# A message-passing layer on one core: the order of VectorE's queue around the message product, and the items in which ranks and node features are made

## The chip, the cores and the metric

The kernel runs on one core of a Trainium2 chip. The metric is device time in microseconds (us), the median of three runs. One more execution was taken by the hardware profiler; its trace is what the profile sections read.

The engines are named as the profile names them: PE is TensorE (PEld its weight loads), DVE is VectorE, ACT is ScalarE, POOL is GpSimd, and SP is the queue that issues most loads.

## The reference

One layer over 6250 nodes and 200000 edges, sorted by the node `dst` from which a message comes.

```python
h = relu(layernorm(x))                                        # 6250 x 128
xw = h @ W_in
W_ij = (ssp(edge_attr @ W_f1 + b_f1) @ W_f2 + b_f2) * edge_weight   # 200000 x 128, ssp(v) = softplus(v) - log 2
x_ij = xw[dst] * W_ij                                         # one message for each edge
out = segment_sum(x_ij, src, 6250)                            # src has no order
return x + ssp(out @ W_o1 + b_o1) @ W_o2 + b_o2
```

## The kernel before

The edges are cut into 391 quads of 4 x 128. One loop iteration, called an item here, works on several quads at different depths. Tiles and semaphores are automatic, but the order of the instructions on each engine is the order in which the program writes them (`manual_schedule`), and each engine takes its instructions in that order. Item `i` is written so:

- PE: `s2_pe_x(i-1)` gathers the node rows of quad `i-1` with a one-hot matrix (tile `xg`) and starts `W`, `s2_pe_w(i-1)` finishes `W`, `s1_pe(i+1)` makes `z`. Then come the hooks "PE2".
- ACT: `s1_exp(i)`, `s1_ln(i)`, hooks "A0", hooks "A1", `s2_copy(i-1)` (four copies of `xg` times the edge weight, tile `xc`), and after PE2 the hooks "A2".
- DVE: hooks "D0", `s1_oh(i)`, hooks "D1", hooks "DM", the message product `s2_m(i-1)` = `W` x `xc` (line 524), and after PE2 the hooks "D2".
- POOL: four indirect DMAs for each quad that is scattered, which add message rows into one of four sums in device memory.

A hook is a step that a planner put at an item and a point with `at(i, point, fn, ...)`; steps at the same item and point run in the order in which they were planned.

184 of the 391 quads are "sorted" quads (`mpq`). They are not scattered one by one. Eight of them and nine others make a round of 17 items; sorted quads stand at the offsets 0, 2, ..., 14 of a round. For a sorted quad `q`:

- item q+1: the product is written to `mb`, then `perm_oh` (D2) builds four one-hot matrices `pm` (line 665);
- item q+2: ACT casts `mb` into `pt` (`part_hi`, line 676, and `part_ext`, line 685, at A1), DVE makes the second part of `pt` (`part_lo`, line 680, at D2);
- items q+3 and q+4: PE permutes `pt` with `pm` (`permute`, line 691), ACT takes the results out (`mst`, line 696); rows over the capacity go through `over_pe`, `over_idx`, `over_row`, `over_eq`, `over_sum`, `over_copy`, `over_ji` (line 753), `over_int` (line 757) and one scatter.

Four "units" follow for each round, at the offsets 2, 6, 10 and 14 of the next one. For a unit at item k, `unit_oh` builds its eight one-hot matrices `so` (line 768), four at k-2 and four at k-1, both at D2; `unit_pe` (line 783) runs 64 matmuls into all four PSUM buffers of tag B; `unit_evac` (line 794) adds them to `accT` in D1 of item k+1. Whatever else PE writes to a tag B buffer in item k+1 waits for that.

`pos`, which `perm_oh` compares with, comes from the "ranks" of a round: `rank_group` (lines 597 to 610, DVE), `rank_count` (lines 615 and 619, PE), `rank_own` (lines 630 to 635, DVE), `rank_over` (PE) and `rank_slot` (lines 648 to 658, DVE).

The other quads are scattered. Most are "listed": a window of 16 of them gets its row numbers ahead from `l_eq` (line 373, a DM hook), `l_count` (line 382), `l_dup`, `l_scan`, `l_index` and others, and closes with `l_sum`, `l_copy`, `l_ji` (lines 484 and 485) and `over_int`.

The node rows are made on the way, in 24 groups of 256 nodes, nine items apart: `prep_stat` (lines 189 to 193, DVE), `prep_rs0` (ACT), `prep_norm` (lines 207 to 213, DVE), `prep_tp` (line 222, PE, tile `hps`), `prep_relu` (ACT), `prep_mm` (PE), `prep_x1` (ACT), `prep_rm` (line 247, DVE), `prep_x2` (line 252, ACT) and `prep_x3` (line 258, DVE, with the store to the table). The edge features are split on the way too, every eight items: `fb_1` to `fb_4`.

`clear(i, busy, n)` gives the first item from `i` on, from which `n` items hold no unit. The tail after the loop adds the sums and makes the output.

## Time and profile before

| | |
|---|---|
| median of 3 runs | 2111.23 us (2109.82 to 2115.32) |
| the profiled execution | 2102.09 us |
| its span (first to last instruction) | 2100.2 us |
| mean granted TensorE clock | 0.932 |
| busy: DVE, ACT, POOL | 1762.2, 1537.2, 1601.1 us |
| busy: PE, PEld | 1786.8, 1532.4 us |
| items of the loop begin at | about 30 us (head), end at about 2030 us (then the tail) |

A busy PE in this table is a union of matmul times whose ends are modelled. "Waits" in the profile are idle time of an engine in front of an instruction, put down to what ended last.

### The profile page before, as it was taken

How to read it: one execution, taken by the hardware profiler on the slowest of the kernel's cores; microseconds unless marked ns; L12 is line 12 of the kernel's file. 1: busy time of each engine (PE TensorE's matmuls, PEld its weight loads, DVE VectorE, ACT ScalarE, POOL GpSimd, SP SyncE). 2: the span in 40 equal slices, each digit the busy share in tenths (PEclk: the TensorE clock that was granted, in tenths of full speed). 3: DMA queues.
4: the chain of work that ended last, by engine and by line, in shares of the span. 5: the costliest groups of instructions: out<-in, count | busy, mean ns of one | idle time of the engine just before them, and what ended most of it. 6: DMA issues, size and time to landing. Idle time of an engine off the chain costs nothing. (4 is left out here: it accounts for less than half of the span.)

```text
span 2100.2 us, 52738 instructions
## 1 busy us (share of the span) xinstructions
PE 1786.8 (85%) x17881; PEld 1532.4 (73%) x17881; DVE 1762.2 (84%) x4448; ACT 1537.2 (73%) x4392; POOL 1601.1 (76%) x984
## 2 busy tenths in 40 slices
PE   3579888887987898988988888888999899998966
PEld 2468777776776777877777777777777777887854
DVE  5687988898888898988989889798898888989865
ACT  3568777776776777777778687687877788898824
POOL 3557888786876877788787788788888888888844
PEclk9789999998999999989999999899999999999978
DMA  7886666665765666666676667666666666767649
GB/s 247 213 202 116 131 117 108 132 107 108 127 119 98 126 124 116 107 118 119 125 125 119 115 110 130 104 118 119 119 118 128 109 117 103 132 116 143 113 87 241
DMA packets 378865, 269.16 MB, mean 128 GB/s; under 512 B 96959, under 2 KB 342506, under 8 KB 378594
## 3 DMA queue, kind: packets, MB, share of 16 engines
q1 hardware_dynamic: 242642, 198.09, 33.7%
q0 software_dynamic: 135664, 67.63, 33.0%
q8 instruction: 141, 2.31, 0.5%
q14 instruction: 130, 1.06, 0.2%
q10 hardware_dynamic: 288, 0.07, 0.0%
HBM read 155.30 MB, written 110.31 MB: 126 GB/s over the span
## 5 line engine op out<-in xcount | busy, mean ns | idle before, releaser
L586 POOL DMA_INDIRECT acc<-s,lji x704 | 1180.3, 1677 | 297.3 <-issue 165.3
L514 ACT ACTIVATE xc<-xg,cb 128x128 f32<-128x128 f32 x1564 | 445.8, 369 | 94.3 <-PE xg L501 91.1
L691 PE MATMUL pq<-pt,pm 128*128 128x258 f32 x2944 | 471.6, 306 | 40.4 <-DVE pt L680 9.9
L509 PE MATMUL W<-w,a 128*128 128x128 f32 x3128 | 475.3, 297 | 0.0
L691 PEld LDWEIGHTS pq<-pt,pm 128*128 128x128 f32 x2944 | 401.6, 200 | 66.9 <-ACT mst L696 12.8
L509 PEld LDWEIGHTS W<-w,a 128*128 128x128 f32 x3128 | 398.4, 200 | 43.6 <-issue 5.9
L783 PE MATMUL un<-so,mst 32*128 32x392 f32 x5888 | 346.8, 368 | 60.9 <-DVE pr L630 40.0
L783 PEld LDWEIGHTS un<-so,mst 32*128 32x128 f32 x5888 | 294.1, 199 | 111.4 <-DVE pr L630 44.8
L665 DVE TENSOR_SCALAR pm<-iot,pos 128x576 fp32r<-128x576 f16 x736 | 345.1, 529 | 0.0
L696 ACT CAST mst<-pq 128x258 fp32r<-128x258 f32 x736 | 253.2, 373 | 113.5 <-PE pq L691 95.7
L327 ACT ACTIVATE a<-a,con 128x512 f32<-128x512 f32 x391 | 282.5, 723 | 12.8
L586 POOL DMA_INDIRECT acc<-s,ji x124 | 206.8, 1668 | 97.4 <-ACT ji L567 43.0
L768 DVE TENSOR_SCALAR so<-iot,mst 128x392 fp32r<-128x392 f16 x736 | 272.8, 431 | 1.4 <-PE un L783 1.4
L322 ACT ACTIVATE a<-z 128x512 f32<-128x512 f32 x391 | 236.3, 604 | 30.6 <-PE z L317 21.6
L794 DVE TENSOR_TENSOR accT<-un,accT 128x392 f32<-128x392 f32 x352 | 174.0, 555 | 35.1 <-PE un L783 34.7
L524 DVE TENSOR_TENSOR s<-W,xc 128x512 f32<-128x512 f32 x176 | 120.8, 687 | 95.0 <-ACT xc L514 87.5
L586 POOL DMA_INDIRECT acc<-os,oji x103 | 172.5, 1675 | 35.4 <-issue 17.7
L501 PE MATMUL xg<-wn,oh 63*128 63x128 bf16 x1564 | 160.2, 225 | 19.4 <-ACT xc L514 13.1
L705 PE MATMUL po<-pt,pm 128*64 128x130 f32 (+1 forms) x736 | 143.1, 251 | 37.7 <-ACT mst L696 24.0
L317 PE MATMUL z<-ft,ws 123*128 123x512 bf16 x391 | 154.3, 395 | 18.3 <-DMA ft<-fsd 15.3
L498 PE MATMUL W<-b2rep,onesb 64*128 64x512 bf16 x391 | 157.1, 402 | 0.0
L705 PEld LDWEIGHTS po<-pt,pm 128*64 128x64 f32 (+1 forms) x736 | 120.7, 168 | 47.2 <-ACT mst L696 29.8
(207 smaller groups left out, 2493.8 us busy)
## 6 DMA issues: line engine op xcount, KB each, us to landing
rb<-reld SPq DMA_DIRECT2D x391, 64.0 KB
fsd<-f SPq DMA_DIRECT2D x49, 480.0 KB
sb<-src SPq DMA_DIRECT2D x183, 128.0 KB
ft<-fsd SPq DMA_DIRECT2D x195, 120.0 KB
fb<-in_fB_dram SPq DMA_DIRECT2D x49, 320.0 KB
ft<-fsd SPq DMA_DIRECT2D x195, 80.0 KB
wn<-tab SPq DMA_DIRECT2D x782, 15.8 KB
acc<-s,lji POOLq DMA_INDIRECT x704
```

Source lines behind the costliest of these rows:

```text
L322: nc.scalar.activation(a, st[q]["z"], AF.Exp)
L327: nc.scalar.activation(a, a, AF.Ln, bias=half, scale=0.5)
L509: nc.tensor.matmul(W[:, c, :], st[q]["a"][:, c * P:(c + 1) * P], w2, start=False, stop=(c == 3))
L514: nc.scalar.mul(xc[:, c, :], st[q]["xg"][:, c, :], late["c", q // CQ][:, 4 * (q % CQ) + c:4 * (q % CQ) + c + 1])
L586: nc.gpsimd.indirect_dma_start(out=accs[k][:rows, :], out_offset=bass.IndirectOffsetOnAxis(ap=ji, axis=0), in_=s, in_offset=None, compute_ ...
L665: nc.vector.tensor_scalar(pm[:, c], iot[:, :SLOTS], rk[r]["pos"][:, 4 * j + c:4 * j + c + 1], None, op0=ALU.is_equal)
L691: nc.tensor.matmul(t[:, :PW], mp[q]["pm"][:, c, s * P:(s + 1) * P], pt[:, c], start=(c == 0), stop=(c == 3))
L696: nc.scalar.copy(mp[q]["ms", s], mp[q].pop(("q", s))[:, :PW])
L705: nc.tensor.matmul(o[:, :P + 2], w, pt[:, c, P:PW], start=(c == 0), stop=False)
L768: nc.vector.tensor_scalar(so, iotw[:, :GN], w[:, 2 * P:2 * P + 1], None, op0=ALU.is_equal)
L783: nc.tensor.matmul(ts[g][:, :GN], mp[q]["ms", s][v, k * P:(k + 1) * P], mp[q]["oh"][v], start=(q == qs[0] and k == 0), stop=(q == qs[-1] a ...
L794: nc.vector.tensor_tensor(v, t[:, :GN], v, op=ALU.add)
```

## The change

Every DVE step planned at "D2" now runs in front of DM and the product instead of after PE2. The first half of each unit's one-hot matrices goes to a new point "D3", at the old place of D2; the second half stays at D2 and so moves in front. `over_ji`, `l_ji` and `over_int` run one item later (D0 and A1 of item k+2). The node steps get two starts, `t0` and `t1`, both at items that are neither a unit nor next to one (`calm`), and are pulled apart: the transpose at t0, the matmul at t1, `prep_x2` at A1 of t1+2, `prep_x3` at D0 of t1+3, the load two items earlier. The ranks are planned at such items too: `rank_count` at k, `rank_over` at o. `rank_group`, which stood at offset 12 of a round, stands at offset 11; `rank_count` moves from offset 13 to 12, `rank_over` from 15 to 16. `over_row` and most `l_count` use `calm` as well. Some small tiles (`ldg`, `leq`, `bb`, `wabs`, `wsel`) move from the tags `h` and `rm`, which the node steps use with one buffer, to a tag of their own with three. The loop has two more items at its end.

```diff
-        dg = wk.tile([P, P], F32, tag="h", name="ldg", bufs=1)
+        dg = wk.tile([P, P], F32, tag="eql", name="ldg", bufs=3)
...
-            t0 = prep_start(g)
-            at(t0 - 3, "L", xt_load, g)
-            at(t0 - 1, "D2", prep_stat, g)
-            at(t0, "A1", prep_rs0, g)
-            at(t0, "D2", prep_norm, g)
-            at(t0 + 1, "PE2", prep_tp, g)
-            at(t0 + 2, "A0", prep_relu, g)
-            at(t0 + 2, "PE2", prep_mm, g)
-            at(t0 + 3, "A0", prep_x1, g)
-            at(t0 + 3, "DM", prep_rm, g)
-            at(t0 + 3, "A2", prep_x2, g)
-            at(t0 + 3, "D2", prep_x3, g)
+            t0, t1 = prep_start(g)
+            at(t0 - 5, "L", xt_load, g)
+            at(t0 - 2, "D2", prep_stat, g)
+            at(t0 - 1, "A1", prep_rs0, g)
+            at(t0 - 1, "D2", prep_norm, g)
+            at(t0, "PE2", prep_tp, g)
+            at(t0 + 1, "A0", prep_relu, g)
+            at(t1, "PE2", prep_mm, g)
+            at(t1 + 1, "A0", prep_x1, g)
+            at(t1 + 1, "DM", prep_rm, g)
+            at(t1 + 2, "A1", prep_x2, g)
+            at(t1 + 3, "D0", prep_x3, g)
...
-            i = max(mpq[RKQ * r], 5)
-            at(i - 5, "D2", rank_group, r)
-            k = clear(i - 4, units)
+            i = mpq[RKQ * r]
+            if i < 10:
+                k, o = i - 1, i
+            else:
+                k = max(k for k in range(i - 20, i - 4) if calm(k, units) == k and calm(k + 1, units) <= i)
+                o = calm(k + 1, units)
+            at(k - 1, "D2", rank_group, r)
             at(k, "PE2", rank_count, r)
             at(k + 1, "D0", rank_own, r)
-            k = clear(k + 1, units)
-            at(k, "PE2", rank_over, r)
-            at(k + 1, "D0", rank_slot, r)
+            at(o, "PE2", rank_over, r)
+            at(o + 1, "D0", rank_slot, r)
...
-            at(k + 1, "DM", l_ji, w)
-            at(k + 1, "A2", over_int, ("L", w))
+            at(k + 2, "D0", l_ji, w)
+            at(k + 2, "A1", over_int, ("L", w))
...
-                k = clear(q + 6, units)
+                k = clear(q + 6, units) if q == mpq[-1] else calm(q + 6, units)
                 at(k, "PE2", over_row, q)
                 at(k + 1, "D0", over_eq, q)
-                k = clear(q + 8, units)
+                k = clear(k + 2, units)
                 at(k, "PE2", over_sum, q)
                 at(k + 1, "A0", over_copy, q)
-                at(k + 1, "DM", over_ji, q)
-                at(k + 1, "A2", over_int, q)
+                at(k + 2, "D0", over_ji, q)
+                at(k + 2, "A1", over_int, q)
...
-                at(k - 2, "D2", unit_oh, r, s, 0)
+                at(k - 2, "D3", unit_oh, r, s, 0)
                 at(k - 1, "D2", unit_oh, r, s, 1)
...
-        for i in range(max(NQ + 7, last + 16, r0_end + 2, lend + 24)):
+        for i in range(max(NQ + 7, last + 18, r0_end + 2, lend + 24)):
...
             run(i, "A1")
             if 0 <= i - 1 < NQ:
                 s2_copy(i - 1)
+            run(i, "D2")
             run(i, "DM")
             if 0 <= i - 1 < NQ:
                 s2_m(i - 1)
...
             run(i, "PE2")
             run(i, "A2")
-            run(i, "D2")
+            run(i, "D3")
...
+def calm(i, busy):
+    while i in busy or i + 1 in busy or i - 1 in busy:
+        i += 1
+    return i
...
-    return clear(7 + PREP_GAP * (g - 1), busy, 3) - 1
+    t0 = calm(7 + PREP_GAP * (g - 1), busy)
+    return t0, calm(t0 + 1, busy)
```

More of the change, by code (lines that the diff above doesn't have):

```diff
@@ L465, in l_same @@
     def l_same(j):
-        eq = wk.tile([P, P], F32, tag="rm", name="leq", bufs=1)
+        eq = wk.tile([P, P], F32, tag="eql", name="leq", bufs=3)
         nc.vector.tensor_scalar(eq, mp["L", j].pop("row")[:, :P], idl[:, j:j + 1], None, op0=ALU.is_equal)
@@ L1015, in tile_gnn @@
             at(t0 + 1, "D2", fb_4, b)
-        busy = units | {prep_start(g) + k for g in range(1, NG) for k in range(5)}
+        busy = units | {t + k for g in range(1, NG) for t in prep_start(g) for k in range(2)}
         mid = clear(NQ // 2, busy, 2) - 6 if spread else 0
@@ L1027, in late_bias @@
             nc.vector.tensor_scalar(nbo1, bo1_sb, -1.0, None, op0=ALU.mult)
-            bb = wk.tile([P, 1, P], F32, tag="rm", name="bb", bufs=1)
+            bb = wk.tile([P, 1, P], F32, tag="eql", name="bb", bufs=3)
             nc.vector.tensor_copy(bb[:, 0], bo1_sb.to_broadcast([P, P]))
@@ L1037, in bound_abs @@
         def bound_abs():
-            t_ = wk.tile([K1, P], F32, tag="h", name="wabs", bufs=1)
+            t_ = wk.tile([K1, P], F32, tag="eql", name="wabs", bufs=3)
             nc.scalar.activation(t_, w1f, AF.Abs)
-            v_ = wk.tile([K1, P], F32, tag="rm", name="wsel", bufs=1)
+            v_ = wk.tile([K1, P], F32, tag="eql", name="wsel", bufs=3)
             nc.vector.tensor_copy(v_, con[:K1, 15:16].to_broadcast([K1, P]))
@@ L1127, in tile_gnn @@
                     at(i + k, "DM", l_eq, kk)
-                i = clear(i + 2, units)
+                i = calm(i + 2, units) if w and g < 3 else clear(i + 2, units)
                 at(i, "PE2", l_count, (LB + SW * w) // 4 + g)
@@ L1509, in base_caps @@
             for g in range(1, len(groups)):
-                if prep_start(g) + 3 >= 2 * s - 4:
+                if prep_start(g)[1] + 3 >= 2 * s - 4:
                     ready = groups[g][0]
```

## The prediction

> **What bounds the kernel now.** First the page's busy times and its row of the granted clock.

> ```profile
> PE 1786.8 (85%) x17881; PEld 1532.4 (73%) x17881; DVE 1762.2 (84%) x4448; ACT 1537.2 (73%) x4392; POOL 1601.1 (76%) x984
> PEclk9789999998999999989999999899999999999978
> ```

> No engine is full. PE and DVE tie at 84 to 85%; head and tail are emptier, so in the loop each is near 88%. The chain that ended last is no help: its rows sum to a few per cent and lie in the tail. So the time is set by two engines handing work to each other, and the question is who waits for whom. That is the table of waits:

> ```profile
> DVE s L524 <- ACT xc L514: 87.5, 84, 3.8
> ...
> ACT oji L757 <- DVE ojd L753: 62.1, 41, 3.6
> ...
> PE un L783 <- DVE pr L630: 40.0, 17, 5.0
> ...
> DVE x L258 <- ACT x L252: 39.4, 15, 4.1
> ...
> PE hps L222 <- DVE accT L794: 26.6, 14, 4.6
> ...
> DVE m L524 <- ACT xc L514: 24.5, 16, 6.5
> ...
> DVE mb L524 <- ACT xc L514: 18.3, 23, 1.9
> ```

> Columns: total us, times, longest. DVE's product waits for the scaled copy 87.5 + 24.5 + 18.3 = 130.3 us, in 123 of 391 items. Each of the other rows belongs to a step that the change moves. Then the stretches: two long ones, and two short ones behind a PE wait of the fifth row.

> ```profile
> 120.00:600.00 480.00, 416.91 (x4114) 360.06 (x4115) 411.05 (x1080) 363.48 (x1047) 371.57 (x223) 0.92 0.66 123
> ...
> 1600.00:2030.00 430.00, 397.29 (x4198) 347.15 (x4202) 372.77 (x910) 334.85 (x980) 355.14 (x215) 0.97 0.66 115
> ...
> 427.00:430.70 3.70, 0.96 (x19) 0.71 (x18) 3.70 (x8) 2.14 (x7) 3.09 (x3) 1.00 0.43 36
> 430.70:434.10 3.40, 3.37 (x19) 2.93 (x17) 3.40 (x8) 2.37 (x7) 2.85 (x2) 0.50 0.57 105
> ```

> Columns: PE, PEld, DVE, ACT, POOL busy, granted clock, DMA share, GB/s. In the early stretch, with node steps, PE idles 63 of 480 us and has a clock of 0.92; in the last, without them, 33 of 430 and 0.97. The two short rows show why these go together: PE was idle for most of 3.7 us, and the next 3.4 us have half the clock. The line of the PE timeline there is

> ```profile
> 429.75 0.44 PE L222 MATMUL hps<-idt,xn 128*128 128x128 f32 x2 [2.71 <-DVE accT L794]
> ```

> In the trace's clock record I count 42 such drops between 120 and 2030 us, 218 us together. Eight follow a wait of `hps` for `accT`, eleven stand at a unit of offset 14, where `un` waits for `pr` (2.9 us at 669 us, for one).

> In rounds: from 156.9 to 1121.6 us eleven rounds take 87.7 us each, with about two node groups in a round; from 1205.2 to 1693.6 us six rounds without node groups take 81.4 us.

> **The change, part by part.** The sum is made against the profiled execution, 2102.1 us; the median of the runs, 2111.2, is 9 us above it. Durations:

> ```profile
> L514 ACT ACTIVATE xc<-xg,cb 128x128 f32<-128x128 f32 x1564 | 445.8, 369 | 94.3 <-PE xg L501 91.1
> ...
> L665 DVE TENSOR_SCALAR pm<-iot,pos 128x576 fp32r<-128x576 f16 x736 | 345.1, 529 | 0.0
> ...
> L768 DVE TENSOR_SCALAR so<-iot,mst 128x392 fp32r<-128x392 f16 x736 | 272.8, 431 | 1.4 <-PE un L783 1.4
> ...
> L680 DVE TENSOR_TENSOR pt<-mb,pt 128x512 fp32r<-128x512 f32 x184 | 125.7, 683 | 0.0
> ...
> L676 ACT CAST pt<-mb 128x512 fp32r<-128x512 f32 x184 | 114.0, 620 | 0.9 <-DVE mb L524 0.6
> ```

> *(a) The new order on DVE.* No instruction of weight is added; the product is only queued later. Gain: where it waited, other work now runs. In the item after a sorted quad's product, `part_lo` (0.68 us) stands in front of the next product. Of the 84 waits of `s` (mean 1.04 us) some 20 lie at offset 0, which has no `part_lo`, and keep theirs; the other 64 lose about 0.6 us each, 38 us. `mb`'s 18.3 go wholly under `perm_oh` (345.1 / 184 = 1.88 us). Of `m`'s 24.5 I take 10. Together 66 us.

> Price: a cover is lost. Before, `perm_oh` and often four `so` (272.8 / 184 = 1.48 us) ran on DVE after `mb`, while ACT cast it, and ACT's cast waited for `mb` 0.6 us in the whole run. Now `mb` comes last, 1.9 to 3.4 us later, and ACT's queue stands: cast 0.62, `ext` 0.20, then `xc` (four, 1.14 us in the timeline), 2.0 us until the next product may start. DVE has for that time `part_lo` and some 0.4 us of small steps: 0.9 us is exposed in each of 184 pairs, 166 us at most. What else now stands there takes part of it back: half of the 88 `eql` (1.2 us each), half of the 49 `fb_2` (1.6) and the 24 `prep_stat` (1.0) cover up to 0.9 us each, 92 x 0.9 = 83. The other 83, and 31 us kept at offset 0 (20 waits, 1.57 us on average there), are 114 against 130 now, -16. The ends: -66 if ACT is always ahead and nothing is newly exposed, +36 if nothing covers (166 - 130). **I take -5**, nearer to the upper end than -16, since the ring also holds `exp` up.

> The late product costs PE little. The buffer that `W` of quad j takes was in the built program last held by `W` of quad j-2 in 337 of 390 cases, so PE needs the product of two items ago. The first half of a unit's `so` keeps its place, the second half comes sooner, and the unit waits for it anyway.

> *(b) Node steps.* `prep_x3` stood right behind ACT's `prep_x2`, which stood behind four `xc`; DVE stood for it 39.4 us, with `pm` and `so` for the next unit queued behind. Now the copy is made at A1 an item earlier than x3. That wait goes; DVE is not always the late one, so I take half: **-20**, ends 0 and -39. The transpose leaves the item after a unit; that wait (26.6) goes, but the buffers are free no sooner: the next tag B user there, `permute`, waits instead. `prep_norm` (1.4 us) leaves the unit's item, `prep_stat` (1.0 us) enters it. **-5**, ends +5 and -27. The loads go out two items earlier on SP's queue, in a space of two buffers that was free: nothing. The store goes from D2 of t0+3 to D0 of t1+3, up to four items later; the table is read far behind: nothing.

> *(c) Ranks.* `rank_own` no longer holds a tag B buffer that a unit needs: 40.0 us of PE waits go. But `rank_group` (seven steps, 3.0 us in the timeline at 1011.4) moves to offset 11, where `accT` (2.0) and `perm_oh` (1.9) stand ahead of the product too; that product becomes 3 us later, and behind it on ACT the cast and `xc`, behind those PE's next `xg`. By hand from one unit's end to the next I get the block no shorter than before. **-4**, ends -40 and +46 (23 rounds x 2.0).

> *(d) Late indices.* ACT loses a wait of 62.1 us with `exp` queued behind. ACT is busy 73%, so most of it was slack: **-4**, ends 0 and -30 (half). The one scatter behind it is written at the same item, and POOL waited for it 1.4 us before; it may now wait up to half an item, 103 times at most, with POOL 76% busy: nothing taken, +10 as an end.

> *(e) Clock.* If the eight drops behind `hps` and half of the eleven at offset 14 go, 13 x 5.2 us (218 / 42) at half clock return 13 x 2.6 = 34 us of PE work; PE is the late one for a part of that: **-8**, ends 0 and -34.

> *(f)* Separate buffers for the small tiles: nothing waits on them now but `leq`, 3.7 us: 0. Two more short items in the tail: **+2**.

> Sum: -5 -20 -5 -4 -4 -8 +2 = **-44**: 2058 on the profiled execution, 2067 as the median.

> [...]

> **The rivals.** *Slower: the lost cover.* One mechanism: product last, ACT's cast and copies, next product, in a ring without slack. If DVE sets the pace nearly everywhere, (a) is +36, the ring also delays `exp` and so PE, and (b) to (e) give back half of theirs, some 20: 2102 + 36 - 20 = 2118, as a median 2127. It decides when DVE's waits for the first cast and for `xc` pass together 130 + 39 = 169 us: the waits before plus the gains of (b) to (f). For it: ACT idles only 27%; against it: the 83 us of other work that now stands in the ring.

> *No change: the ranks eat it.* (c) near its end of +46 cancels the -40 of the rest: 2111. For it: PE's `un` waits follow DVE's whole load, which stays.

> *Much faster.* PE's waits go for good, and the clock of the whole loop is that of the last stretch: 13.6% of the time at half clock now, 6% then, 80 us of PE work, of which I count half, with (a) at -30: 2102 - 40 - 30 - 33 (b to d) + 2 = 2001 at the extreme, 2010 as a median; I give it the middle between that and the forecast, 2038.

> *The drops stay.* They come from PE's load over a window, not from the two waits; then (e) is 0: 2075 as a median. For it: several drops stand behind no wait over 1 us. [...]

> **How the numbers follow.** Forecast 0.47 (its own range 2040 to 2098), lost cover 0.23, ranks 0.08, much faster 0.14, drops stay 0.08. A measurement can tell about 0.3%, 6 us. Faster: 0.47 + 0.14 + 0.08, less 0.01 for the forecast's upper end: 0.68. Slower: 0.23. Same: 0.09. The range from 2028 to 2126 leaves out about half of the lost-cover case above and a third of the fastest below.

> **What would show it.** Right: `x <- ACT x`, `oji <- ojd` and `un <- pr` gone from the waits; the product's waits for `xc` near 110 us; a new wait of DVE's `pt` for ACT's cast, of 30 to 80 us; a granted clock near 0.94; rounds with node groups near 85 us. The lost cover shows as `pt` and `s` waits over 169 us and ACT idle in front of its cast of `mb`. The ranks show as PE or ACT idle at offsets 12 to 14. The forecast is wrong if DVE's idle time does not fall, or if it falls and rounds do not shorten.

## The result, and the profile after

The changed kernel is slower: median 2234.11 us (2230.23 to 2241.87, four runs) against 2111.32 us for the kernel before, run beside it; ratio 1.0583, 95% interval 1.0551 to 1.0615. The forecast was 2067 us in a range of 2028 to 2126. The profiled execution took 2230.23 us, its span 2228.4 us, its mean granted clock was 0.891.

The page's busy times, its clock row, and the windows of the loop in the changed kernel (columns as in the prediction):

```profile
PE 1816.0 (81%) x17881; PEld 1579.3 (71%) x17881; DVE 1783.3 (80%) x4448; ACT 1535.6 (69%) x4392; POOL 1581.2 (71%) x984
PEclk9789889898998988989888899898989998999987
```

```profile
120.00:600.00 480.00, 395.79 (x3871) 345.95 (x3870) 394.67 (x1029) 340.01 (x986) 350.84 (x212) 0.88 0.63 119
...
1600.00:2160.00 560.00, 497.53 (x5177) 436.03 (x5177) 471.18 (x1139) 416.34 (x1208) 436.48 (x263) 0.93 0.63 109
```

The instruction counts are those of before, and the busy times of PE, DVE, ACT and POOL moved by 29 us at most. PE, at 0.88 instead of 0.92 in the first stretch, was also idle for 84 us there instead of 63. So the 128 us that the span has grown are mostly waiting, and a slower clock behind it. The table of waits of the changed kernel says for whom:

```profile
ACT dg L725 <- DVE ovs L720: 147.1, 60, 5.6
...
DVE pt L680 <- ACT pt L676: 139.7, 93, 5.4
ACT mst L696 <- PE pq L691: 114.2, 102, 4.1
...
PE po L705 <- ACT mst L696: 70.2, 40, 4.1
...
DVE s L524 <- ACT xc L514: 59.0, 92, 4.1
...
ACT pt L676 <- DVE mb L524: 41.5, 29, 3.0
```

The rows that the prediction wanted gone are gone or small (`un <- pr` and `hps <- accT` gone, `x <- ACT x` 0.5 us, `oji <- ojd` 12.0). In their place stands a first row that the prediction does not have: ACT waits 147.1 us, in 60 places, for `ovs`. Before, that row was a small one:

```profile
ACT dg L725 <- DVE ovs L720: 9.2, 16, 1.5
```

`ovs` is `over_idx`, a DM step of one tiny DVE instruction, and `dg` is `over_dg`, the first hook (A0) of the next item on ACT.

One place of it, in item 12 of a round; DVE, ACT and PE by the timeline (start, duration, and in brackets the idle time in front and its releaser):

```profile
1157.59 0.18 DVE L597 CAST srcf<-srcT_sb 128x32 f32<-128x32 int16 x1
...
1159.87 0.18 DVE L610 CAST ext<-cnt 128x32 bf16<-128x32 f32 x1
1159.95 1.80 DVE L665 TENSOR_SCALAR pm<-iot,pos 128x576 fp32r<-128x576 f16 x4
1161.67 0.15 DVE L720 SCALAR_TENSOR_TENSOR ovs<-mo 128x1 f32<-128x1 f32 x1
```

```profile
1161.86 0.40 ACT L725 ACTIVATE dg<-idt,ovs 128x128 f32<-128x128 f32 x1 [4.55 <-DVE ovs L720]
1162.16 0.28 ACT L728 ACTIVATE ojd<-ovs,con 128x1 f32<-128x1 f32 x1
1162.35 0.62 ACT L696 CAST mst<-pq 128x258 fp32r<-128x258 f32 x2
```

```profile
1162.75 0.38 PE L615 MATMUL rkp<-G,tri 128*128 128x512 bf16 x1 [3.24 <-ACT mst L696]
...
1168.12 2.50 PE L691 MATMUL pq<-pt,pm 128*128 128x258 f32 x8 [4.33 <-DVE pr L630]
```

The chain: seven rank steps and four `pm` (4.1 us) now run on DVE in front of DM; the 0.15 us of `ovs` come behind them; ACT stands 4.55 us in front of `dg`, and in its queue behind `dg` are the `mst` that empty PE's tag B buffers; PE stands 3.24 us for a buffer, later 4.33 us more, until DVE's `pr` has freed the buffer of the ranks' own count; and then, at a granted clock of 0.50, the eight `pq` take 2.50 us, where eight of them take 1.20 us at a granted clock of 1.00 (at 1156.22 us of the same trace).

The length of an item, from the start of one `W` to the next, is worked out from the trace (mean of the rounds 2 to 20, us, by offset in the round; last column: time at half clock between 120 and 2030 us). The rows below `after` are experiments:

| kernel | 4 | 8 | 12 | 16 | all 17 | half clock |
|---|---|---|---|---|---|---|
| before | 3.8 | 4.3 | 4.7 | 4.6 | 84.1 | 218 |
| after | 6.1 | 7.0 | 11.5 | 8.5 | 90.5 | 403 |
| e2 | 5.0 | 5.4 | 7.9 | 6.9 | 85.2 | 239 |
| e8 | 3.9 | 4.7 | 4.9 | 4.7 | 83.2 | 222 |
| e10 | 4.0 | 4.7 | 4.8 | 4.6 | 82.0 | 215 |
| e16 | 4.2 | 5.7 | 5.6 | 5.4 | 82.7 | 215 |
| e6 | 6.2 | 6.4 | 6.6 | 5.9 | 85.5 | 276 |
| e1 | 6.2 | 6.2 | 11.0 | 7.8 | 88.6 | 362 |
| e9 | 3.6 | 4.7 | 9.5 | 7.1 | 85.1 | 249 |
| e13 | 3.9 | 4.8 | 8.3 | 5.5 | 84.1 | 249 |
| e14 | 3.7 | 4.7 | 7.2 | 6.3 | 83.2 | 259 |

The whole loss lies in four items of a round: 4, 8, 12 and 16 are together 15.7 us longer than before, the other thirteen 9.3 us shorter. These are the items that `calm` returns: with units at 2, 6, 10 and 14, only 0, 4, 8, 12 and 16 are neither a unit nor next to one. They are also the items of `q+4` for the sorted quads at offsets 0, 4, 8 and 12, in which PE2 already makes the second half of a permuted quad and its overflow, three tag B results that ACT takes out only at A0 of the next item. The change puts into just these items the ranks' counts (from 13 and 15), most `l_count` and the nodes' `hps` (both from the odd offsets). Of the four `over_row` of a round three stood at 8, 12 and 16 before; the fourth goes from 3 to 4.

### The profile page after: what moved, and what is told of

Same layout as the page of the kernel before. It is cut to its first block, busy times and chain, and to the rows that moved or that the text cites. A ratio compares the mean times of both kernels' runs of the same rounds, so it can differ in the third digit from the quotient of the medians.

```text
span 2228.4 us, 52670 instructions
## 1 busy us (share of the span) xinstructions
PE 1816.0 (81%) x17881; PEld 1579.3 (71%) x17881; DVE 1783.3 (80%) x4448; ACT 1535.6 (69%) x4392; POOL 1581.2 (71%) x984
## 5 line engine op out<-in xcount | busy, mean ns | idle before, releaser
L586 POOL DMA_INDIRECT acc<-s,lji x704 | 1165.5, 1656 | 420.8 <-issue 161.3
L691 PE MATMUL pq<-pt,pm 128*128 128x258 f32 x2944 | 497.5, 318 | 94.6 <-ACT h L228 32.3
L509 PE MATMUL W<-w,a 128*128 128x128 f32 x3128 | 510.6, 313 | 0.0
L691 PEld LDWEIGHTS pq<-pt,pm 128*128 128x128 f32 x2944 | 425.4, 210 | 119.6 <-ACT mst L696 36.9
L514 ACT ACTIVATE xc<-xg,cb 128x128 f32<-128x128 f32 x1564 | 443.8, 367 | 34.3 <-PE xg L501 27.2
L509 PEld LDWEIGHTS W<-w,a 128*128 128x128 f32 x3128 | 430.1, 213 | 46.9 <-issue 13.1
L665 DVE TENSOR_SCALAR pm<-iot,pos 128x576 fp32r<-128x576 f16 x736 | 343.7, 528 | 9.9 <-PE po L706 7.7
L783 PE MATMUL un<-so,mst 32*128 32x392 f32 x5888 | 296.4, 345 | 2.6 <-DVE oeq L738 1.1
L783 PEld LDWEIGHTS un<-so,mst 32*128 32x128 f32 x5888 | 263.0, 184 | 38.4 <-issue 28.9
L768 DVE TENSOR_SCALAR so<-iot,mst 128x392 fp32r<-128x392 f16 x736 | 277.5, 437 | 1.9 <-PE un L783 1.7
L680 DVE TENSOR_TENSOR pt<-mb,pt 128x512 fp32r<-128x512 f32 x184 | 127.2, 691 | 159.3 <-ACT pt L676 139.7
L705 PE MATMUL po<-pt,pm 128*64 128x130 f32 (+1 forms) x736 | 160.2, 274 | 93.4 <-ACT mst L696 70.2
L705 PEld LDWEIGHTS po<-pt,pm 128*64 128x64 f32 (+1 forms) x736 | 135.2, 187 | 107.7 <-ACT mst L696 80.2
L794 DVE TENSOR_TENSOR accT<-un,accT 128x392 f32<-128x392 f32 x352 | 174.4, 558 | 30.8 <-PE un L783 16.7
L524 DVE TENSOR_TENSOR s<-W,xc 128x512 f32<-128x512 f32 x176 | 121.3, 689 | 78.6 <-ACT xc L514 59.0
L501 PE MATMUL xg<-wn,oh 63*128 63x128 bf16 x1564 | 168.3, 234 | 18.7 <-ACT xc L514 16.9
```

What stands on the lines that cost most here:

```text
L509: nc.tensor.matmul(W[:, c, :], st[q]["a"][:, c * P:(c + 1) * P], w2, start=False, stop=(c == 3))
L514: nc.scalar.mul(xc[:, c, :], st[q]["xg"][:, c, :], late["c", q // CQ][:, 4 * (q % CQ) + c:4 * (q % CQ) + c + 1])
L586: nc.gpsimd.indirect_dma_start(out=accs[k][:rows, :], out_offset=bass.IndirectOffsetOnAxis(ap=ji, axis=0), in_=s, in_offset=None, compute_ ...
L665: nc.vector.tensor_scalar(pm[:, c], iot[:, :SLOTS], rk[r]["pos"][:, 4 * j + c:4 * j + c + 1], None, op0=ALU.is_equal)
L691: nc.tensor.matmul(t[:, :PW], mp[q]["pm"][:, c, s * P:(s + 1) * P], pt[:, c], start=(c == 0), stop=(c == 3))
L705: nc.tensor.matmul(o[:, :P + 2], w, pt[:, c, P:PW], start=(c == 0), stop=False)
```

## The experiments

Two theories. *The late index*: the order "D2 in front of DM" makes `over_idx` late, and ACT and PE behind it. *The lost cover*, the prediction's rival: the product last, ACT's cast and copies and the next product form a ring without slack, whatever stands at DM. The parts that the change plans anew (ranks, nodes) could add to either. Each ratio is to runs of the kernel before that were made together with it.

### The order on DVE: e1, e2, e3, e4, e8

```diff
 # e1 (on the changed kernel) and e8 (on e3): the DM hooks first
-            run(i, "D2")
             run(i, "DM")
+            run(i, "D2")
             if 0 <= i - 1 < NQ:
                 s2_m(i - 1)
 # e2: the changed kernel, all of D2 behind PE2 again
 # e3: the kernel before, and only the new order
+            run(i, "D2")
             run(i, "DM")
...
-            run(i, "D2")
+            run(i, "D3")     # first half of unit_oh, prep_x3
 # e4: the kernel before, and over_idx alone behind D2
-                at(q + 5, "DM", over_idx, q)
+                at(q + 5, "D3", over_idx, q)
```

> The changed kernel with DM in front of D2 again, so that over_idx, l_eq, l... and prep_rm run ahead of the one-hot matrices and ranks, while the product stays behind all of them. Theory 'late index' (over_idx fell behind D2, ACT's dg waits for it 147 us with all of ACT queued behind): that wait falls under 20 us and the time to 2100-2140 us. Theory 'lost cover' (product last, then ACT's cast, then pt): dg recovers but pt's wait for the cast stays over 100 us and the time stays over 2190. Theory 'ranks at offset 11': the time stays over 2190 and the long PE gaps stay at offset 12.

> The changed kernel with D2 back behind the product and PE2; node steps, ranks, late indices and buffers stay changed. 'Late index' and 'lost cover' alike: both costs gone, and what is left are the other parts, forecast at -40 us: 2060-2100. 'Ranks at offset 11': stays over 2150.

> The kernel before with only the place of D2 changed (first half of a unit's matrices and prep_x3 stay at the old place). 'Late index': dg waits over 100 us for ovs, time 2190-2260. 'Lost cover': dg waits little, pt waits over 100 us, time 2150-2260. 'Ranks at offset 11': the old rank places are kept, so 2100-2130.

> The kernel before, with over_idx alone moved from in front of the product to behind all of D2 (92 small DVE instructions). 'Late index': dg waits over 100 us, time 2160-2230. 'Lost cover' and 'ranks': within 10 us of 2111.

> The kernel before with D2 in front of the product and DM in front of D2: the place alone, without the late index. 'Late index': the 70 us of dg waits go and the time falls from 2137 to 2095-2115. 'Lost cover': the product is as late as before, 2125-2145.

| | median, us | ratio (95%) |
|---|---|---|
| e1, changed, DM first | 2185.55 | 1.036 (1.0327 to 1.0393) |
| e2, changed, D2 at its old place | 2119.73 | 1.0037 (1.0016 to 1.0058) |
| e3, only the order | 2137.02 | 1.0135 (1.0105 to 1.0166) |
| e4, only `over_idx` late | 2211.6 | 1.0484 (1.0447 to 1.052) |
| e8, only the order, DM first | 2077.68 | 0.9847 (0.9805 to 0.9889) |

e1 puts `over_idx` back in front: `dg` then waits for `ovs` 1.6 us in 2 places, and 47 us of the 123 come back. That leaves 2185.55 us, where 2100 to 2140 were expected if the late index were all.

e4 moves 92 instructions of 0.15 us in an otherwise untouched kernel, further back than the change does, and costs 100 us. Its table of waits:

```profile
DVE s L524 <- ACT xc L514: 136.2, 81, 3.7
...
ACT dg L725 <- DVE ovs L720: 129.5, 64, 4.8
```

e3 and e8 differ in the place of DM alone: 2.9% of 2111, 61 us. In e3 `dg` waits 70.3 us for `ovs`; a wait over 100 us and a time of 2190 us or more were expected, so the late index costs less there than the theory said. Not all of the 61 us need be `over_idx`: `over_ji`, `l_ji`, `l_eq` and `prep_rm` stand at DM too, and ACT's wait of `oji` for `ojd` is 82.4 us in e3 and 14.0 in e8. And e8, in which the product is still the last step on DVE, is faster than the kernel before. Its waits:

```profile
ACT pt L676 <- DVE mb L524: 93.4, 81, 4.0
...
DVE pt L680 <- ACT pt L676: 27.4, 38, 3.3
...
DVE s L524 <- ACT xc L514: 24.8, 42, 1.9
```

ACT does stand in front of its cast, 93.4 us, as the lost cover said. But DVE's waits for the cast and for `xc` are 27.4 + 24.8 + 3.9 (`m`) = 56.1 us, against 130.3 for `xc` before and the 169 at which the rival would decide. On the old plan the ring has slack, and the order itself is a gain of 1.5%.

On the new plan it is not so. In the changed kernel the same rows make 139.7 + 59.0 + 5.3 = 204 us, and in e1, with the index on time, 109.3 + 59.0 + 6.0 = 174 us: the rival's mark is passed in both. e1 and e2 differ in one thing, whether D2 stands in front of the product or behind PE2, and e1 is 3.2 points slower, 68 us. So D2 in front of the product gains 32 us on the old plan and costs 68 us on the new one; whether the crowded items make this difference is the question of e13 to e18. The order as a whole (e2 to the changed kernel) is 5.5 points, 115 of the 123 us. The rest of the change, on the old order, is 0.4 points slower than the kernel before, where 2060 to 2100 us were expected; its items 12 and 16 are long even so (7.9 and 6.9 us), with 239 us at half clock.

### The parts that are planned anew: e5, e6, e7, e9, e10, e11, e12, e16

e5 is the changed kernel and e6 is e1, both with the old rank plan; e7 is the changed kernel with the old node plan. e9, e10 and e11 are e8 with one part each: the new rank plan; the late indices; the new node plan with the tag of its own for the small tiles. e16 is e10 with that of e11. e12 is the changed kernel with `rank_group` behind the product.

```diff
 # e9 (and, the other way round, e5 and e6)
-            i = max(mpq[RKQ * r], 5)
-            at(i - 5, "D2", rank_group, r)
-            k = clear(i - 4, units)
+            i = mpq[RKQ * r]
...
+                k = max(k for k in range(i - 20, i - 4) if calm(k, units) == k and calm(k + 1, units) <= i)
+                o = calm(k + 1, units)
+            at(k - 1, "D2", rank_group, r)
 # e10
-                at(k + 1, "DM", over_ji, q)
-                at(k + 1, "A2", over_int, q)
+                at(k + 2, "D0", over_ji, q)
+                at(k + 2, "A1", over_int, q)
 # e11 and e16 (and, the other way round, e7): the prep_* lines of the change
-            t0 = prep_start(g)
+            t0, t1 = prep_start(g)
 # e12
-            at(k - 1, "D2", rank_group, r)
+            at(k - 1, "D3", rank_group, r)
```

> The changed kernel with the old places of the ranks (rank_group at offset 12, rank_count 13, rank_over 15), the rest as changed. Theory 'ranks in front at offset 11' (3 us of rank_group stand behind accT and ahead of pm, the late index and the product, so ACT's dg and cast wait, and PE behind ACT): dg's wait for ovs falls from 147 to about 70 us, the clock drops at offsets 12 and 16 thin out, time 2150-2190. Theory 'lost cover': the product is last either way, time stays over 2210.

> DM in front of D2 and the old places of the ranks; the product is still behind all of D2. 'Ranks' and 'late index' together explain the loss: 2100-2130. 'Lost cover': stays over 2160, with pt waits near 110 us.

> The changed kernel with the old node plan (prep_x3 at the old place). If the node steps gathered at items 4, 8, 12, 16 of a round are part of the loss, 2190-2215; if not, 2230-2260, since x3's wait for x2 (29 to 39 us) comes back.

> e8 (old plan, D2 and DM in front of the product, DM first) with the new places of the ranks alone. If the ranks at offset 11 cost what e5 gave back (75 us) by themselves: 2135-2160, with clock drops at offsets 12 and 16. If they cost only by the late index standing behind them: 2075-2095.

> e8 with l_ji, over_ji and over_int one item later, alone. If the late indices gain as forecast: 2065-2078. If D0 and A1 an item later only move a wait: 2078-2095, with ACT's oji waiting again.

> e8 with the new node plan and the separate small buffers, alone. If the node plan gains as forecast (x3's 17 us wait goes, PE's first tag B user after a unit is free): 2050-2075. If it costs what e7 gave back (30 us): 2095-2115, the slow rounds being those up to item 220.

> The changed kernel with rank_group alone moved from in front of the product to behind it, at the same offset 11. If standing in front of the product and the late index is what costs: 2234 falls to 2150-2180, as in e5. If the offset itself costs (a full item): stays over 2200.

> The best version so far (product last behind the lists, late indices an item later, 2059.5 us) with the changed kernel's node places and separate small tags added. On the kernel without the late indices the node places brought nothing (2077.6 against 2077.7 us). Theory 'nodes are free where the product is on time': 2052 to 2065 us, the waits of x for x, 39 us before, gone without a shorter time. Theory 'the nodes add to the late indices' (both free DVE and ACT at the head of an item): 2040 to 2052 us. If nodes cost what they cost in the changed kernel, 30 us: about 2090 us.

| | median, us | ratio (95%) |
|---|---|---|
| e5, changed, old ranks | 2159.36 | 1.0217 (1.0171 to 1.0264) |
| e6, changed, DM first, old ranks | 2126.98 | 1.0067 (1.0042 to 1.0092) |
| e7, changed, old nodes | 2203.54 | 1.0451 (1.0409 to 1.0493) |
| e9, e8 and new ranks | 2122.07 | 1.0074 (1.0045 to 1.0103) |
| e10, e8 and late indices | 2059.48 | 0.9781 (0.9758 to 0.9804) |
| e11, e8 and new nodes | 2077.63 | 0.9879 (0.9852 to 0.9907) |
| e12, changed, `rank_group` behind | 2181.59 | 1.0373 (1.0345 to 1.04) |
| e16, e10 and new nodes | 2075.79 | 0.9882 (0.9849 to 0.9916) |

These make a ladder from the kernel before to the changed one, each step one part, in points of the ratio and in us of 2111:

| step | ratio | points | us |
|---|---|---|---|
| before to e8: product last, DM in front | 0.9847 | -1.5 | -32 |
| e8 to e10: late indices | 0.9781 | -0.7 | -14 |
| e10 to e16: nodes, separate tags | 0.9882 | +1.0 | +21 |
| e16 to e6: `over_row` and `l_count` at calm items (with `over_sum` and the longer loop) | 1.0067 | +1.9 | +39 |
| e6 to e1: ranks | 1.036 | +2.9 | +62 |
| e1 to the changed kernel: DM behind D2 | 1.0583 | +2.2 | +47 |

Steps between runs that were not made together carry the uncertainty of two ratios, some 0.3 to 0.5 points. The order in which the parts are put in decides their shares: D2 in front of the product is the first step here, -32 us, and would be +68 between e2 and e1. The parts are not additive: the nodes cost 0.3 points on e8, within that uncertainty, 1.0 on e10 and 1.3 in the changed kernel; the ranks 2.3 on e8 and 3.7 in the changed kernel. The fourth step was not run alone; it is the difference of two kernels. The ranges expected for e9, e10, e11, e15 and e16 were missed: e9, e11 and e15 came out between the theories, e16 beside all three, and e10 faster than either.

e12 returns 2.1 of the 3.7 points of the ranks in the changed kernel: so much hangs there on the rank steps in front of `over_idx` and the product. The counts keep their new items in it, and items 12 and 16 still take 9.3 and 8.4 us.

The gain of e10 is not the one that was forecast. The wait that the late indices were to remove is 14.0 us in e8, where they are not late, and in e10 it is back:

```profile
ACT oji L757 <- DVE ojd L753: 56.4, 35, 4.4
```

In e2, on the old order, it is 81.1 us, against 62.1 before. What makes e10 faster than e8 by 0.7 points is not shown.

e10 is the fastest of all: 2.2% faster than the kernel before, 7.6% faster than the changed one by the ratios (0.9781 / 1.0583).

### Why the calm items cost: e13, e14, e15, e17, e18

In e9 the index is on time, and items 12 and 16 are still 9.5 and 7.1 us. One item 12 there, on ACT and on PE:

```profile
1434.27 0.62 ACT L676 CAST pt<-mb 128x512 fp32r<-128x512 f32 x1 [2.97 <-DVE mb L524]
...
1437.36 0.63 ACT L696 CAST mst<-pq 128x258 fp32r<-128x258 f32 x2
```

```profile
1431.78 0.38 PE L615 MATMUL rkp<-G,tri 128*128 128x512 bf16 x1
1432.00 0.49 PE L619 MATMUL rkp<-G,onesb 128*128 128x384 bf16 x3
1432.33 0.44 PE L733 MATMUL orow<-dg,onesf 128*128 128x128 f32 x2
1432.52 0.72 PE L691 MATMUL pq<-pt,pm 128*128 128x258 f32 x4
1434.43 0.75 PE L691 MATMUL pq<-pt,pm 128*128 128x258 f32 x4 [1.19 <-DVE ldup L389]
1437.76 0.37 PE L705 MATMUL po<-pt,pm 128*64 128x130 f32 x1 [2.58 <-ACT mst L696]
```

PE makes `rkp`, `orow` and two `pq` (the last only after `ldup` has freed the `lcnt` of the item before), and these are all four buffers; `po` would be the fifth. The buffers come free when ACT reaches `mst` of the next item, and ACT had stood 2.97 us for an `mb` that the seven rank steps (2.4 us) and `pm` in front of it made late. Two things meet: the crowded item and the late product. The runs take one or the other away:

```diff
 # e13 (e9, at the items of the counts) and e15 (e1) and e17 (e10), both at all items:
 # the second half is taken out behind its matmuls
-                    at(q + 4 + s // 2, "A0", perm_out, q, s)     # s = 2, 3
-                at(q + 5, "A0", over_out, q)
+                        at(q + 4, "PE2", perm_out, q, s)
+                at(q + 4, "PE2", over_out, q)
 # e14: e8, with a one-column tag B result at offsets 12 and 16
+                at(i, "PE2", fifth, i)
+                at(i + 1, "D0", fifth_read, i)
 # e18: e9, the rank steps behind the product of offset 10
-            at(k - 1, "D2", rank_group, r)
+            at(max(k - 2, 0), "D3", rank_group, r)
```

> The product last behind the lists, with the new rank places (2122 us as it stood), and one more edit: in the items that make the ranks' counts (offsets 12 and 16) the second half of a permuted quad and its overflow are taken out by ACT right behind their matmuls, not at the head of the next item, so that no tag B buffer with them is held into the next item. Theory 'buffers' (in these items PE lacks a tag B buffer until ACT, late by its wait for mb, has taken out the quad before): 2080 to 2095 us; the 103 us of waits of po for mst fall under 50; the 17 clock drops at offset 12 fall under 8. Theory 'late product' (seven rank steps in front of the product make everything behind it late, whatever the buffers): 2115 to 2125 us, the drops stay.

> The product last behind the lists, old places of ranks and nodes (2077.7 us as it stood), and in each round, at offsets 12 and 16, one dummy matmul of a single column into a tag B buffer, first of the hooks PE2, read by a one-column copy of DVE at the head of the next item. It adds no work of weight (46 matmuls and 46 copies, some 5 to 8 us in sum). Theory 'buffers': one more held buffer in these items costs by itself 20 to 45 us: 2095 to 2120 us, with clock drops in items 12 and 16. Theory 'late product': 2078 to 2086 us.

> The changed kernel with the DM hooks in front of the D2 steps (2185.6 us as it stood), and the second half of every permuted quad and of its overflow taken out by ACT right behind the matmuls, in all items. Theory 'buffers': much of what the new ranks and nodes cost comes back, 2080 to 2130 us. Theory 'late product': ACT only does the same copies at another place, 2165 to 2195 us.

> The best version (product last behind the lists, late indices an item later, 2059.5 us, ratio 0.978), and in all items the second half of a permuted quad and its overflow taken out by ACT right behind the matmuls, as in the changed kernel with the lists in front, where that gave 47 us. Theory 'buffers held while ACT is late': here ACT is on time in the items 12 and 16, so nothing comes of it, ratio 0.974 to 0.984. If taking out early helps in itself, whatever the ranks: ratio under 0.972, and then the 25 and 47 us say nothing of the ranks. If ACT then stands for PE's matmuls of the same item, ratio over 0.986.

> The product last behind the lists with the new rank places (2122 us, ratio 1.0074 as it stood), but the seven rank steps behind the product of offset 10 (D3) instead of in front of the product of offset 11; the counts keep their new items 12 and 16, and no buffer is freed. Theory 'buffers alone' (one more tag B result in the items 12 and 16): stays near 1.0, at least 0.995, as with the dummy result plus what is held longer. Theory 'late product sets it off, the buffers only pass it on': falls to 0.986 to 0.992, near the dummy result's 0.990; items 12 and 16 of 6.5 to 7.5 and 5.5 to 6.5 us instead of 9.5 and 7.1.

| | median, us | ratio (95%) | against |
|---|---|---|---|
| e13, e9 with buffers freed | 2097.49 | 0.9961 (0.9939 to 0.9982) | e9 1.0074 |
| e14, e8 with a held result | 2082.74 | 0.9898 (0.9866 to 0.9931) | e8 0.9847 |
| e15, e1 with buffers freed | 2138.77 | 1.0169 (1.0134 to 1.0203) | e1 1.036 |
| e17, e10 with buffers freed | 2067.11 | 0.9806 (0.9774 to 0.9837) | e10 0.9781 |
| e18, e9 with the rank steps earlier | 2106.68 | 0.9994 (0.9971 to 1.0017) | e9 1.0074 |

Freeing the buffers returns 1.1 and 1.9 points where ACT is late, and nothing where it is on time (e17), so it is not a gain in itself. In e13 item 16 is nearly short again (5.5 us, 1 drop of the clock there instead of 15), but item 12 is not (8.3 us, 15 drops instead of 17). In e9, e13 and e14 the row of PE's wait for a buffer reads

```profile
PE po L705 <- ACT mst L696: 103.2, 40, 5.2
```

```profile
PE po L705 <- ACT mst L696: 69.5, 48, 3.7
```

```profile
PE po L706 <- ACT mst L697: 58.5, 34, 4.5
```

and it is 31.7 us in e8. For e13 less than 50 us was expected of the theory of the buffers. A held buffer alone (e14) makes the items 12 and 16 longer by 2.3 and 1.6 us against e8, with ten drops of the clock at each, but the rest of the round takes all but 0.5 points of it back: the 20 to 45 us expected for it were too much. Rank steps that stand earlier and behind a product (e18) return only 0.8 points, less than the 1.5 to 2.1 that the theory of the late product expected; they then lengthen item 11 instead (6.2 us against 4.2 in e10). So neither explanation carries the ranks' cost alone. Of the 2.3 points on e8, about half is shown to hang on the buffers; that the other half is the 2.4 us of rank steps, at whatever place they stand in front of ACT's cast, is argued from the timelines and stays open.

## Why the prediction was wrong

**(a), the step that failed first.** "No instruction of weight is added; the product is only queued later" is false: everything at DM is queued later too. The prediction weighed the moved steps and the product, and not the other steps that D2 now passes, one of which, `over_idx`, feeds the first hook of ACT's next item. DM behind D2 is 47 us in the changed kernel and 61 us on the kernel before with nothing but the new order. The table of waits before had the row (`dg <- ovs`, 9.2 us in 16 places): what became the largest wait of the changed kernel stood there as a small number, because DVE reached `over_idx` early.

The rest of (a), the product behind D2, was forecast at -5 between -66 and +36. Alone (e8) it is -32; on the new plan (e1 against e2) it is +68. Two things went wrong in it. The gains of (a) to (d) were added as if they were separate, but the order alone takes most of their waits: in e8 the waits for `xc` fall from 130.3 to 28.7 us, `x` for ACT's `x` from 39.4 to 16.8, `hps` for `accT` from 26.6 to 9.7, `un` for `pr` from 40.0 to 13.5, `oji` for `ojd` from 62.1 to 14.0. And the price of the lost cover was worked out for the items as they were: there DVE waits 27.4 us for ACT's cast, not 83, and in the changed kernel 139.7.

**(b)** -25 was taken, with the ends of the two terms at -66 and +5. The waits went as predicted and no gain came of it: +7 us on e8, within the uncertainty, +21 on e10, +28 in the changed kernel. The sentence that "the next tag B user there, `permute`, waits instead" was the right worry at the wrong item: the transpose was moved into the items whose buffers were already taken. There `pq` and `po` wait 32.3 + 15.0 us, in 20 places, until ACT's `h` has emptied `hps`; before, `pq` waited 2.5 us for it.

**(c)** -4 was taken, with an upper end of +46; it is +48 on e8, +62 in the ladder, +77 in the changed kernel. The wait of `un` for `pr` went, but PE stands for buffers elsewhere (`po` for `mst`, 103.2 us in e9 against 31.7 in e8), so on balance none of the -40 was gained. The end of 2.0 us a round was about right on e8 (85.1 against 83.2 us, e9); in the ladder a round loses 3.1 us, where `l_count` and the nodes are in the same items. The seven rank steps, read as 3.0 us, take 2.4 us in the timeline at 1011.4. By the ladder this is the largest single term.

**(d)** -4, ends 0 and -30: -14 on e8 (e10), inside the ends, but by luck: the wait that was to go is longer in e10 than in e8 (56.4 against 14.0 us).

**(e)** had the wrong sign. Half-clock time grew from 218 to 403 us, as 20 and 18 of 65 drops now stand at the items 12 and 16. By an estimate from the granted clock of 0.50, the 185 us more at half clock are work that takes 92 us at full clock; in the changed kernel eight `pq` took 2.06 to 2.50 us at 0.50 and 1.19 to 1.38 us at 1.00.

**Not costed at all**: `l_count` and `over_row` at calm items (with `over_sum` and the longer loop), 39 us by the ladder. The section on the change names them, and the sum has no term for them: what the new items already hold was not counted.

**The rivals.** The lost cover gave the sign. By its mechanism alone it is refuted (e8), but on the new plan it holds in part: its mark of 169 us is passed, and the late product costs 68 us (e1 against e2), a price that it did not foresee to hang on the new plan of the other parts. "The ranks eat it" named the right step, priced at up to +46 us against 48 to 77 measured. "The drops stay" came true and worse. Its reason, PE's load over a window, was a supposition; what the traces show is that PE was busy for less than 2 us of the last 3.41 us before 103 of the 107 drops in the kernel before and the changed kernel (last section). The drop in the e9 example came inside an idle time of 2.6 us.

## What to carry to other kernels

When a step is moved in an in-order queue, list everything that it passes, and for each the first instruction on another engine that waits for it; in e4, 92 instructions of 0.15 us that stand in front of another engine's queue cost 100 us of the whole when they came late. Before moving work to "quiet" places, count what these places already hold of the resource that is short (here four PSUM buffers), since a rule like "not next to a unit" collects all movers at the same few items. Try an order on the plan that it will run with: the same order gained 32 us on the old plan and cost 68 on the new one. And a wait that disappears is no gain until the next one in line is known: here five rows of the waits went or shrank, and the kernel became 5.8% slower.

## What the runs showed of the hardware that I had not expected

In e9 the clock fell before an idle time of 2.6 us was over. The item 12 of e9 by windows (PE, PEld, DVE, ACT, POOL busy, then the granted clock):

```profile
1432.00:1435.10 3.10, 1.91 (x14) 1.49 (x12) 2.68 (x8) 0.83 (x3) 2.73 (x2) 1.00 0.75 121
1435.10:1437.70 2.60, 0.08 (x1) 0.00 (x0) 2.16 (x5) 2.57 (x9) 2.13 (x2) 0.69 0.29 26
1437.70:1441.00 3.30, 3.24 (x20) 2.92 (x21) 3.23 (x9) 1.69 (x7) 2.85 (x2) 0.50 0.48 45
```

A mean of 0.69 over the idle 2.6 us is 1.6 us at half clock, so the drop came about 1 us after PE's last work; the work behind it then ran at a granted clock of 0.50.
